# Sorting networks of a graph kernel: scalar_tensor_tensor in place of tensor_tensor, over whole 66-column slots

## The chip, the core and the metric

The kernel runs on one core of a Trainium2 chip. A core has a matrix engine (TensorE; PE in the profile, its weight loads PEld), a vector engine (VectorE, DVE), an activation engine (ScalarE, ACT), a general engine (GpSimd, POOL), which here starts the gathers, and SyncE (SP), which starts plain DMAs. Each engine works through its own list of instructions in a fixed order; semaphores order the engines among each other, and also an instruction behind an earlier one of the same engine where the data ask for it. The metric is the device time of one execution in microseconds (us).

## The reference, cut to what matters

Input are 16 batches of a graph with 1024 nodes and 64 channels, with a sparse adjacency matrix (about 16 neighbours to a node). Four layers follow each other, each ending in a residual and a layer normalisation:

- Layer 0: `x + adj @ (x @ W) + b`.
- Layer 1: neighbours are thinned out (a node with more than 10 neighbours loses one or two of them, and they lose it), and then, for every node and channel, the values of the kept neighbours and of the node are **sorted**, and three interpolated quantiles of them are added with weights. A small network of two matrix products follows.
- Layer 2: an embedding, three rounds of `relu(adj @ (h @ W + b))`, and a projection.
- Layer 3: `t = adj @ x`, of which only `t > 0.5` is used.

The sort of layer 1 is what the change touches:

```
vals = jnp.where(valid[..., None], x[:, None, :, :], big)
sv = jnp.sort(vals, axis=2)
...
for tau, wt in zip(TAUS, QWEIGHTS):
    q = gather(lo) * (1.0 - frac) + gather(hi) * frac
    agg = agg + wt * q
```

## The kernel before

**Tiles and groups.** Each batch's 1024 nodes are put into an order by their number of kept neighbours and cut into eight tiles of 128 nodes, one node to a partition. A tile with its longest lists needs 31, 21, 19, 17, 15, 15, 13 or 11 **slots** (`KS`). Tiles are handled in five groups (`GROUPS`): tile 0 alone with 31 slots, tiles 6 and 7 together with 13, tiles 2 and 3 with 19, tiles 4 and 5 with 15, tile 1 alone with 21. A slot of one tile is a row of `R` = 66 float32 columns to a partition: the 64 channels of a neighbour (`C` = 64) and two columns that hold which two neighbours the thinning takes out there. With two tiles in a group their rows for the same slot lie next to each other.

**Steps of one group.** `gathered` (L808) fetches the rows: one indirect DMA on POOL for each slot and tile (L815), 129 to a batch with some shared ones, into a buffer `g` that comes from a ring of four. `masked` (L847) reads the two extra columns (L862) and adds a huge number to rows that don't count, on ACT (L868). `quantiles` (L891) sorts the slots by a **network**: a fixed list of minimum and maximum operations over slots (`NETS`, L72), each one DVE instruction at L906, which goes back and forth between `g` and a second buffer `s`. An entry of the list holds the operation, the buffers, and for each operand a first slot, a run of neighbouring slots, a step and a count of runs. `box` (L898) makes the access pattern of it: up to three dimensions (count, rows of the run, 64 columns), so that the two extra columns are left out. `summed` (L916) weighs the needed sorted slots on ACT (L932) and adds them up on PE (L936).

**The rest of a batch.** `words_of` (L502) loads and transposes the adjacency rows and runs layer 0; on DVE it has L526 and L527. `listing` (L587) makes the lists of neighbours; on DVE it has L646, L694, L699, L701, L707 and L710, among them two with three inputs: L694 with a constant and L710 with one number to a partition. `back` (L1122) runs the small network of layer 1 and layers 2 and 3, mostly on PE, with a layer normalisation (L383) on DVE and ACT.

**What sets the order.** All steps are Python generators that yield a planned duration after each instruction or two. A planner (L1233 to L1271) holds a queue of them by planned time, pops the earliest, lets it emit its next piece and puts it back at its time plus the yielded duration times a stretch. The order of emission is the order on every engine. Batches overlap: the five groups of a batch have planned lengths (`LENGTHS`, 192.06 in sum, the period of a batch), gathers of a group are planned two groups ahead of its network, and `back` of a batch runs beside the networks of the next. The stretch of a network makes its instructions fill the group's length; the planned durations are these:

```
yield (nt * count * run * C + 151) / 960
...
cost = 0.2 + sum((len(GROUPS[g]) * x[4] * x[8] * C + 151) / 960 for x in network(n))
add(start(q), quantiles(st, g), (start(q + 1) - start(q)) / (cost + 0.1))
```

Of the kernel before, what the change touches and what calls it, by code (L numbers as in the profile page):

```python
# [17 lines left out]
ALU = mybir.AluOpType  # L18
# [129 lines left out]

def network(n):
    return [tuple(map(int, op.split(","))) for op in NETS[n].split(";")]  # L150


@with_exitstack
def kernel(
# [18 lines left out]
    nc = tc.nc  # L173
    B, N, C = x.shape
# [7 lines left out]
    R = C + 2  # L182
# [41 lines left out]
    for c in range(T):  # L224
        for s in range(2):
            half = slice(s * W, (s + 1) * W)
            nc.vector.tensor_scalar(pow2[half, c, :W], ident[half, half], 2.0 ** (7 - 2 * c - s),
                                    None, op0=ALU.mult)
# [9 lines left out]
    for t in range(T):  # L238
        n = max(KS[u] for g in GROUPS for u in g if t in g)
# [71 lines left out]
    for i in range(S):  # L311
# [4 lines left out]
        else:  # L316
            nc.vector.scalar_tensor_tensor(bias16, piece, ident[:S, i:i + 1], bias16,
                                           op0=ALU.mult, op1=ALU.add)
# [463 lines left out]
    def group(g):  # L782

        n = max(KS[t] for t in GROUPS[g])
        lo, hi = RANKS[n]
        return GROUPS[g], n, lo, hi + 1 - lo
# [104 lines left out]
    def quantiles(st, g):  # L891
        tiles, n, lo, kw = group(g)
        nt = len(tiles)
        while ("hat", g) not in st:
            yield 0.5
        bufs = st["g", g], srt.tile([P, KMAX * R], F32, tag="y", name="s", bufs=2)

        def box(buf, first, run, step, count):  # L898
            v = buf[:, first * nt * R:]
            dims = [[step * nt * R, count]] if count > 1 else []  # L900
            dims += [[R, run * nt]] if run * nt > 1 else []
            return bass.AP(tensor=v.tensor, offset=v.offset,
                           ap=[list(v.ap[0])] + dims + [[1, C]])

        for mode, a, b, d, run, sa, sb, sd, count in network(n):
            nc.vector.tensor_tensor(box(bufs[mode >> 1 & 1], d, run, sd, count),  # L906
                                    box(bufs[mode >> 3], a, run, sa, count),
                                    box(bufs[mode >> 2 & 1], b, run, sb, count),
                                    ALU.max if mode & 1 else ALU.min)
            yield (nt * count * run * C + 151) / 960  # L910
        w = tmp.tile([P, nt, kw], F32, tag="w", name="w")
        nc.vector.tensor_reduce(w, st["hat", g].rearrange("p t s k -> p t k s"), AX.X, ALU.add)  # L912
        yield 0.2
        st["sorted", g] = bufs, w
# [334 lines left out]
    for b in range(B):  # L1249
        ready = start(b * G - 2) - BEFORE  # L1250
        add(ready - LISTS - WORDS, words_of(state[b]), WORDS / WORDS_STEPS)
        add(ready - LISTS - (LEAD if b else EARLY), front(state[b]), LISTS / LISTS_STEPS)
        add(start((b + 1) * G) + AFTER, back(state[b]), BACK / BACK_STEPS)
        for g in range(G):
            q = b * G + g
            st = state[b]
            count = sum(KS[t] for t in GROUPS[g])
            many = sum(ROWS[t].count(P) for t in GROUPS[g]) + len(packs_of(g))
            add(start(q - 2), gathered(st, g), (start(q - 1) - start(q - 2)) / (many + 1))
            half = (start(q) - start(q - 1)) * (PAIRS if len(GROUPS[g]) > 1 else MASKS)  # L1260
            add(start(q) - half, masked(st, g), 0.9 * half / (1.5 + 0.4 * count + 2.1 * len(GROUPS[g])))
            n = max(KS[t] for t in GROUPS[g])
            cost = 0.2 + sum((len(GROUPS[g]) * x[4] * x[8] * C + 151) / 960 for x in network(n))
            add(start(q), quantiles(st, g), (start(q + 1) - start(q)) / (cost + 0.1))
            add(start(q + 1) + SUMS, summed(st, g))
# [50 lines left out]
```

## Time and profile before

| | |
|---|---|
| time, median of 3 runs | 3176.69 us (3176.14 to 3177.83) |
| span of the profiled execution | 4328.2 us; the page gives no other time for it |
| busy PE, DVE, ACT, POOL in it | 2647.8, 2822.0, 1914.0, 2160.8 us |
| mean granted TensorE clock | 0.764 |
| network instructions (L906) | 3648, which is 228 to a batch |
| gathers of slots (L815, `g<-table`) | 1952, mean 1048 ns, median 947 ns |

The profiled execution is 1151.5 us longer than the median of the runs. Its rows tell what an instruction takes and what holds it; how full the engines are in an ordinary run has to be worked out by setting busy times against 3176.69 us. Busy is the union of the instructions' durations, so that instructions of one engine that overlap count once. In groups of instructions, `s<-g 128x768` means that an instruction writes 768 elements in each of 128 partitions of `s` from data in `g`.

### The profile page before, as it was taken

The page shows a single profiled execution, that of the slowest core. Times are in us where ns is not written, and L with a number is a line of the kernel's source. Part 1 is how long each engine was busy: PE and PEld are TensorE (multiplying, and loading weights), DVE is VectorE, ACT ScalarE, POOL GpSimd, SP SyncE. Part 2 cuts the span into 40 slices and gives each one's busy share as a digit, 9 for nine tenths or more (in the row PEclk, how much of TensorE's full clock was granted, in tenths as well). Part 3 has the DMA queues.
Part 4 walks back from the last instruction along what each step waited for, and adds up shares of the span by engine and source line. Part 5 has one row for each costly group of instructions (what it writes and reads, how often), then busy time and mean ns, then how long its engine had stood idle before and what let it go on. Part 6 is the DMA issues. An engine that isn't in the chain of part 4 may idle for free.

```text
span 4328.2 us, 46055 instructions
## 1 busy us (share of the span) xinstructions
PE 2647.8 (61%) x13765; PEld 1635.7 (38%) x13766; DVE 2822.0 (65%) x6935; ACT 1914.0 (44%) x6153; POOL 2160.8 (50%) x2078
## 2 busy tenths in 40 slices
PE   6034285675848567584755758476575848456478
PEld 5023152443525244352533435253343525233243
DVE  6058383865849486594857668485766859476671
ACT  2034352634536264453535455363545536253641
POOL 1715626455454645546465464546545554645600
PEclk8566597787969778796877879687787969768688
DMA  3212121322222132222213222231322222111210
GB/s 107 42 50 70 34 67 37 104 54 78 73 71 84 40 101 56 78 77 74 77 39 90 64 83 76 65 84 40 100 60 79 78 80 71 39 57 24 62 43 3
DMA packets 169056, 282.54 MB, mean 65 GB/s; under 512 B 99485, under 2 KB 102112, under 8 KB 166880
## 3 DMA queue, kind: packets, MB, share of 16 engines
q1 hardware_dynamic: 67584, 142.01, 9.9%
q0 software_dynamic: 66048, 69.88, 9.1%
q10 hardware_dynamic: 35168, 67.62, 4.1%
q8 instruction: 114, 1.87, 0.2%
q14 instruction: 142, 1.16, 0.1%
HBM read 204.33 MB, written 71.44 MB: 64 GB/s over the span
## 4 chain that ended last, share of the span: by engine, by line
another core or an unknown queue 28%; DVE 25%; PE 23%; ACT 16%; issue 7%; DMA 0%; ACTq 0%; DVEq 0%
DVE g L906 7%; PE mm L1207 7%; DVE s L906 7%; ACT g L868 6%; ACT ones_at L974 3%; PE ax L464 3%; ACT ones_at L975 2%; PE tp L439 2%; PE mm L377 2%; PE pa L936 2%; PE mm L1196 2%; ACT g L932 1%; PE mm L1141 1%; DVE top L707 1%
## 5 line engine op out<-in xcount | busy, mean ns | idle before, releaser
L815 POOL DMA_INDIRECT g<-table,idx x1952 | 2045.4, 1048 | 1919.7 <-PE pa L936 666.8
L1207 PE MATMUL mm<-adjB,msg 128*128 128x512 f32 x1536 | 769.6, 621 | 109.1 <-issue 82.4
L936 PE MATMUL pa<-g,ident 128*128 128x128 f32 (+1 forms) x1600 | 376.0, 360 | 430.1 <-ACT g L932 300.5
L868 ACT ACTIVATE g<-g,bias 128x64 f32<-128x64 f32 (+9 forms) x2272 | 596.8, 341 | 47.9 <-DVE bias L864 29.2
L906 DVE TENSOR_TENSOR s<-g 128x256 f32<-128x256 f32 (+9 forms) x944 | 531.3, 588 | 64.5 <-ACT g L868 55.5
L936 PEld LDWEIGHTS pa<-g,ident 128*128 128x128 f32 x1600 | 312.3, 248 | 574.0 <-ACT g L932 347.1
L906 DVE TENSOR_TENSOR g<-s 128x256 f32<-128x256 f32 (+8 forms) x864 | 473.4, 573 | 9.0 <-DVE s L906 3.0
L932 ACT ACTIVATE g<-g,w 128x64 f32<-128x64 f32 x1552 | 397.8, 341 | 17.2 <-DVE w L912 13.6
L1207 PEld LDWEIGHTS mm<-adjB,msg 128*128 128x128 f32 x1536 | 268.7, 197 | 301.1 <-issue 270.7
L1147 DVE TENSOR_TENSOR u<-mm,mb 128x512 f32<-128x512 f32 x32 | 22.1, 691 | 463.1 <-remote 313.5
L464 PE MATMUL ax<-at,xt 128*64 128x128 f32 x1920 | 284.5, 310 | 17.4 <-issue 17.4
L377 PE MATMUL mm<-adjB,x 128*64 128x512 f32 x512 | 272.6, 666 | 36.3 <-issue 31.3
L979 PE MATMUL mm<-ones_at,pieces 128*64 128x512 bf16 x768 | 213.0, 420 | 119.0 <-ACT ones_at L975 77.1
L464 PEld LDWEIGHTS ax<-at,xt 128*64 128x64 f32 x1920 | 250.2, 158 | 81.2 <-issue 79.1
L439 PE MATMUL tp<-ident,arow 128*128 128x128 f32 x1024 | 181.7, 309 | 156.2 <-remote 66.4
L399 DVE TENSOR_REDUCE ln_v<-sq 128x8 f32<-128x512 f32 x64 | 43.6, 681 | 296.4 <-issue 156.8
L439 PEld LDWEIGHTS tp<-ident,arow 128*128 128x128 f32 x1024 | 140.9, 162 | 205.1 <-issue 131.7
L441 ACT COPY at<-tp 128x512 f32<-128x512 f32 x240 | 139.0, 580 | 177.2 <-remote 122.3
L906 DVE TENSOR_TENSOR g<-g,s 128x256 f32<-128x256 f32 (+5 forms) x432 | 199.1, 464 | 15.1 <-remote 5.0
L906 DVE TENSOR_TENSOR g<-g 128x256 f32<-128x256 f32 (+8 forms) x304 | 200.7, 660 | 11.2 <-remote 4.0
L1219 PE MATMUL mm<-ident,tT 64*128 64x64 f32 x128 | 25.7, 295 | 293.9 <-ACT tT L380 207.4
L1210 ACT ACTIVATE hlT<-mm 128x512 f32<-128x512 f32 x96 | 57.4, 598 | 296.4 <-PE mm L1207 123.7
(225 smaller groups left out, 4361.9 us busy)
## 6 DMA issues: line engine op xcount, KB each, us to landing
arow<-in_adj_dram SPq DMA_DIRECT2D x128, 512.0 KB
adjd<-at ACTq DMA_DIRECT2D x120, 512.0 KB
adjB<-adjd SPq DMA_DIRECT2D x15, 4096.0 KB
g<-table,idx POOLq DMA_INDIRECT x1952
table<-xc ACTq DMA_DIRECT2D x16, 264.0 KB
xt<-in_x_dram SPq DMA_DIRECT2D x16, 256.0 KB
out_dram<-y SPq DMA_DIRECT2D x16, 256.0 KB
stage<-table,packed POOLq DMA_INDIRECT x112
```

The costliest lines, as they stand in the source:

```text
L377: nc.tensor.matmul(pa[:C, :], src[:, m, :], adjT[:, h * TH:(h + 1) * TH, m, :], start=(m == 0), stop=(m == T - 1))
L439: nc.tensor.transpose(pt[:, i * P:(i + 1) * P], a[:, j * P:(j + 1) * P], ident)
L441: nc.scalar.copy(at[:, h * TH:(h + 1) * TH, :], pt.rearrange("p (i n) -> p i n", n=P))
L464: nc.tensor.matmul(self.bank[:C, cols], self.xt[:, m + 1, :], at[:, m, :], start=(m == 0), stop=(m == T - 1))
L815: nc.gpsimd.indirect_dma_start(out=dst, out_offset=None, in_=st["table"], in_offset=bass.IndirectOffsetOnAxis(ap=index, axis=0))
L868: nc.scalar.activation(v, v, AF.Identity, bias=bias[:m, i, k:k + 1])
L906: nc.vector.tensor_tensor(box(bufs[mode >> 1 & 1], d, run, sd, count), box(bufs[mode >> 3], a, run, sa, count), box(bufs[mode >> 2 & 1], b ...
L932: nc.scalar.activation(slots(g, bufs[0], lo + r, lo + r + 1)[:, i, 0, :C], slots(g, bufs[at[r]], lo + r, lo + r + 1)[:, i, 0, :C], AF.Iden ...
L936: nc.tensor.matmul(pa[:, :(e - k) * nt * C], ident, rows_.rearrange("p (k c) -> p k c", c=R)[:, :, :C], start=(j == 0), stop=(j == len(run ...
L974: nc.scalar.activation(ones_at, iota, AF.Abs, bias=st["minus"][:, s:s + 1])
L979: nc.tensor.matmul(bank[:C, :], pieces[:, i, s, :], ones_at[:, h * HALF:(h + 1) * HALF], start=(s == 0 and i == 0), stop=False)
L1207: nc.tensor.matmul(pg, msg[:, m, :], adjT[:, h * TH:(h + 1) * TH, m, :], start=(m == 0), stop=(m == T - 1))
```

## The change

Each minimum or maximum of a network becomes a `scalar_tensor_tensor` that multiplies the first operand by the constant 1.0 and then takes the minimum or maximum with the second. That instruction gets at most two dimensions beside the partitions here, where the old boxes had up to three. So a box of several runs is taken over all 66 columns of its rows: rows of a run are then one stretch of `run * nt * 66` elements, and the second dimension is the count. A function `widths` goes through a network from its end and gives each operation its width: 66 where it has several runs of more than one row, or where a later operation of width 66 reads what it writes; else 64. The planned duration that a network's step yields goes by the new width; `cost`, from which the stretch is worked out, still goes by 64 columns. The two extra columns of a slot hold no more than leftovers after `masked` has read them, and nothing reads them later but the networks.

```diff
+def widths(n, nt, narrow, full):
+
+    def places(buf, first, run, step, count):
+        return {(buf, first + i * step + r) for i in range(count) for r in range(run)}
+
+    read, found = set(), []
+    for mode, a, b, d, run, sa, sb, sd, count in reversed(network(n)):
+        out = places(mode >> 1 & 1, d, run, sd, count)
+        wide = bool(out & read) or (count > 1 and run * nt > 1)
+        read -= out
+        if wide:
+            read |= places(mode >> 3, a, run, sa, count) | places(mode >> 2 & 1, b, run, sb, count)
+        found.append(full if wide else narrow)
+    return found[::-1]
...
-        def box(buf, first, run, step, count):
+        def box(buf, first, run, step, count, width):
             v = buf[:, first * nt * R:]
-            dims = [[step * nt * R, count]] if count > 1 else []
-            dims += [[R, run * nt]] if run * nt > 1 else []
-            return bass.AP(tensor=v.tensor, offset=v.offset,
-                           ap=[list(v.ap[0])] + dims + [[1, C]])
-
-        for mode, a, b, d, run, sa, sb, sd, count in network(n):
-            nc.vector.tensor_tensor(box(bufs[mode >> 1 & 1], d, run, sd, count),
-                                    box(bufs[mode >> 3], a, run, sa, count),
-                                    box(bufs[mode >> 2 & 1], b, run, sb, count),
-                                    ALU.max if mode & 1 else ALU.min)
-            yield (nt * count * run * C + 151) / 960
+            if run * nt == 1:
+                dims = [[step * R, count]] if count > 1 else []
+                dims += [[1, width]]
+            elif width == R:
+                dims = [[step * nt * R, count]] if count > 1 else []
+                dims += [[1, run * nt * R]]
+            else:
+                dims = [[R, run * nt], [1, width]]
+            return bass.AP(tensor=v.tensor, offset=v.offset, ap=[list(v.ap[0])] + dims)
+
+        for (mode, a, b, d, run, sa, sb, sd, count), width in zip(network(n), widths(n, nt, C, R)):
+            nc.vector.scalar_tensor_tensor(box(bufs[mode >> 1 & 1], d, run, sd, count, width),
+                                           box(bufs[mode >> 3], a, run, sa, count, width), 1.0,
+                                           box(bufs[mode >> 2 & 1], b, run, sb, count, width),
+                                           op0=ALU.mult, op1=ALU.max if mode & 1 else ALU.min)
+            yield (nt * count * run * width + 151) / 960
```

What the networks consist of, for one batch, and how many operations get width 66:

| group of tiles | operations | elements to a partition | of width 66 | elements added |
|---|---|---|---|---|
| 0 | 46 | 22,592 | 44 | 666 |
| 6, 7 | 34 | 11,648 | 34 | 364 |
| 2, 3 | 59 | 23,040 | 58 | 716 |
| 4, 5 | 28 | 14,336 | 28 | 448 |
| 1 | 61 | 13,120 | 59 | 384 |
| a batch | 228 | 84,736 | 223 | 2,578 |

## The prediction

> **What bounds the kernel now.** I read the page first, for what is full and what ended last.
>
> ```profile
> span 4328.2 us, 46055 instructions
> ...
> PE 2647.8 (61%) x13765; PEld 1635.7 (38%) x13766; DVE 2822.0 (65%) x6935; ACT 1914.0 (44%) x6153; POOL 2160.8 (50%) x2078
> ...
> another core or an unknown queue 28%; DVE 25%; PE 23%; ACT 16%; issue 7%; DMA 0%; ACTq 0%; DVEq 0%
> ...
> L815 POOL DMA_INDIRECT g<-table,idx x1952 | 2045.4, 1048 | 1919.7 <-PE pa L936 666.8
> ```
>
> The profiled execution is 1151.5 us longer than the median of the runs, 3176.69 us, and 28% of its span (1212 us) is time on the chain that no engine or known queue accounts for. An ordinary run can't hold that, so idle time here says little about it; busy time says more. The second view, stretches of time, cuts the span before the first network instruction (267) and behind the last (4195):
>
> ```profile
> 0.00:267.00 267.00, 86.77 (x755) 73.69 (x757) 76.81 (x284) 40.88 (x119) 107.17 (x124) 0.68 0.25 66
> 267.00:4195.00 3928.00, 2459.69 (x12692) 1512.10 (x12691) 2726.86 (x6609) 1844.63 (x5983) 2053.64 (x1954) 0.77 0.24 66
> 4195.00:4329.00 134.00, 101.29 (x318) 49.96 (x318) 18.33 (x44) 28.47 (x53) 0.00 (x0) 0.81 0.10 36
> ```
>
> (Length, then busy PE, PEld, DVE, ACT, POOL.) DVE works 2726.9 us between its first and last network instruction. An ordinary run has for that stretch 3176.7 less the 134 us tail, less a head that can't be under about 130 us: the first gather starts at 96 us and the 21 whole slots of tile 0 follow each other by 1.25 us or more. That leaves some 2910 us, 94% of which DVE is busy. I take DVE as what paces an ordinary run. POOL comes close: 2160.8 busy and 0.30 us between gathers, which the view of waits calls issue:
>
> ```profile
> POOL g L815 <- PE pa L936: 666.8, 42, 80.5
> POOL g L815 <- issue: 566.6, 1858, 0.5
> ```
>
> With 96 ahead of the first gather and about 215 behind the last (4114.7 of 4328.2) that makes 2161 + 567 + 311 = 3039 us of 3177. Its other waits are for buffers that the sorted groups free (L936), so it stands behind the networks more than ahead of them.
>
> **The change part by part.**
>
> *The instruction by itself.* Groups of DVE instructions, shapes apart:
>
> ```profile
> L906 DVE TENSOR_TENSOR s<-g 128x768 f32<-128x768 f32 x144 | 136.4, 957 | 1.2
> L906 DVE TENSOR_TENSOR g<-s 128x512 f32<-128x512 f32 x160 | 106.8, 692 | 1.6
> L906 DVE TENSOR_TENSOR s<-g 128x256 f32<-128x256 f32 x256 | 102.0, 420 | 0.7
> L694 DVE SCALAR_TENSOR_TENSOR cand<-wd,wordkey 128x512 int32<-128x512 int32 x75 | 51.4, 686 | 71.0 <-ACT wd L688 40.3 <-issue 22.4 <-ACT hat L886 4.2
> L710 DVE SCALAR_TENSOR_TENSOR kw<-cand,top 128x320 f32<-128x320 f32 x128 | 72.1, 563 | 12.9 <-DVE top L707 7.1 <-remote 1.6
> ```
>
> At 512 elements a scalar_tensor_tensor with a constant (L694) takes 686 ns, a network's tensor_tensor 692. But durations overlap; what counts is from start to start, in the timeline:
>
> ```profile
> 2290.42 0.17 DVE L407 SCALAR_TENSOR_TENSOR ln_v<-ln_v,ln_r 128x8 f32<-128x8 f32 x1
> 2290.62 0.17 DVE L408 SCALAR_TENSOR_TENSOR ln_v<-ln_v,ln_r 128x8 f32<-128x8 f32 x1
> 2290.82 0.17 DVE L409 SCALAR_TENSOR_TENSOR ln_r<-ln_v,ln_r 128x8 f32<-128x8 f32 x1
> 2290.91 0.68 DVE L906 TENSOR_TENSOR s<-g 128x512 f32<-128x512 f32 x1
> 2291.51 0.68 DVE L411 TENSOR_TENSOR y<-u,ln_r 128x512 f32<-128x512 f32 x1
> ```
>
> A 512-element tensor_tensor is followed after 0.60 us (2290.91 to 2291.51). So is L694, below (3087.08 to 3087.68). So 3648 instructions change their kind at a price of nothing. The bounds: L694 against L906 says -6 ns each (-22 us); L710, which takes a number per partition and not a constant, takes 552 ns at its median, some 66 above the 486 of a 320-element tensor_tensor (+241 us in all). L694 is the nearer row, having a constant, and I take zero; but its type is int32, and the only float32 rows with a constant and two buffers (L407 to L409) have 8 elements.
>
> One rule speaks against this part. The Trainium skill, Vector Engine (DVE) Microarchitecture Reference, section 7, says that such an instruction with two non-bf16 sources in SBUF runs at half throughput. By it the 1,397,024 elements of the changed networks would cost about 1,455 us more, an estimate, and the kernel would take about 4,630 us. The trace differs: at two cycles of 1.04 ns for each of 320 elements L710 would last over 667 ns, and it takes 552; L694 would take twice its time.
>
> *The extra columns.* 223 of a batch's 228 operations get width 66, 2,578 elements to a batch, 41,248 in all. The slope from the rows: (957 - 420) / (768 - 256) = 1.05 ns. That is 43 us of DVE time, in the networks, with no cover on DVE itself. Old three-dimensional boxes pay nothing for their extra dimension (692 ns at 512, like the plain 693 of L701 of that size), so the simpler pattern gives nothing back.
>
> *Waits among DVE instructions.* In the built programs the network instructions that wait for the one directly ahead of them on DVE go from 1168 to 1251, since boxes that didn't touch now do in the columns between. The price: L408 starts 0.20 us behind L407, for which it waits; the network instruction that doesn't wait starts 0.09 behind L409. Rows of 256 elements say 0.45 against 0.335. So 0.115 us each, 83 times, 10 us. What is queued behind each is the next DVE instruction. Waits for ACT stay at 87.
>
> *The gathers.* While POOL starts a gather inside a DVE instruction with two inputs, the gather lasts until that instruction ends:
>
> ```profile
> 2048.54 1.40 DVE L906 TENSOR_TENSOR g<-g,s 128x512 f32<-128x512 f32 x2
> 2048.67 1.35 POOL L815 DMA_INDIRECT g<-table,idx  x1 [0.30 <-issue]
> ...
> 3087.08 0.69 DVE L694 SCALAR_TENSOR_TENSOR cand<-wd,wordkey 128x512 int32<-128x512 int32 x1
> 3087.42 1.17 POOL L815 DMA_INDIRECT g<-table,idx  x1 [0.30 <-issue]
> 3087.68 0.42 DVE L699 TENSOR_SCALAR bit<-wd 128x512 int32<-128x512 int32 x1
> ```
>
> An unheld gather takes 947 ns (the median). The first began 0.13 us into a 0.67 us tensor_tensor and took 0.40 more; the second began 0.34 into a 0.69 us scalar_tensor_tensor and took 0.22 more: they end 0.81 and 0.82 us behind that instruction's end. So the new kind holds gathers just as the old one. All holding adds 1952 x (1048 - 947) = 197 us to POOL, some 165 of it by networks; a wait's mean length goes with the square of the instruction's, 1.03 x 1.03, so +10 us on POOL, beside DVE's work.
>
> *The order.* POOL and SP keep theirs. On DVE, PE and ACT steps trade places by a few, since network steps are planned up to 3% longer (2.7 us to a batch, times a stretch of 1.0 to 1.9) while `cost` stays; a network's end, and with it `summed`, is planned about a microsecond later. I put this at nothing, from -10 to +15 us: it moves what DVE does next, not what it does, and the cover is that both lists keep DVE fed.
>
> The sum on DVE is 43 + 10 = 53 us. With DVE idle for 6% of its stretch, and idle time at a group's first operations able to swallow more than its share, I let 85% through: **+45 us, 3222 us**. In the profiled execution L906 holds 7.4 + 7.1% of the chain, 628 us of the 1971 that its instructions last, so its own span would grow by a third of 53, some 17 us, to 4345; its unexplained stretches can hide that.
>
> **The rivals.**
> *POOL paces.* Then DVE's 53 us fall into idle time and +10 remains: 3187, up to 3200 where both alternate. For it: 3039 of 3177. Against: 42 waits for L936.
> *Gathers run free.* The constant's form with float32 lets go of what the gather needs. Then POOL loses up to 165 us, and as far as it paces the kernel gets faster, down to DVE's floor: 130 + 2727 + 53 + 134 = 3044, likelier about 3110. It decides if gathers that start inside network instructions come to 0.95 us. Against: L694 and L710 hold them to their ends.
> *Covered.* DVE's waits swallow it all: 3170 to 3183. Against: 94%.
> *Order goes bad.* Displaced steps make another engine wait: +15 us and more on top, 3240 to 3290.
> *Half throughput*: 4,630 by the page cited; from the rows alone at most 241 + 53, 3470.
>
> **How the numbers follow.** DVE paces, 3205 to 3238: 0.66. POOL paces, 3184 to 3200: 0.14. Covered: 0.06. Gathers free: 0.05. Order bad: 0.06. A dearer instruction (half throughput or L710's extra): 0.03. The order may also turn out lucky, 0.02 out of the first. Runs of this kernel tell 0.2% (6.4 us) from no change. Faster 0.07, same 0.06, slower 0.87. The range 3182 to 3246 holds the first two cases and some of the fourth, 8 in 10.
>
> **What would show it.** Right: network rows of 264, 528 and 792 elements at about 428, 709 and 982 ns as SCALAR_TENSOR_TENSOR; DVE busy up by some 45; gathers at a mean of 1050 to 1060 ns, those inside a network instruction still held to its end. Wrong: network rows of another slope, gathers at 950, or DVE idle behind ACT or PE where it now follows itself.

## The result and the profile after

The changed kernel takes 3224.62 us (median of 4 runs, 3223.05 to 3228.91), the kernel before beside it 3176.41 us (4 runs, 3174.85 to 3177.83). The ratio is 1.0153, with a 95% interval of 1.0139 to 1.0168: 48.2 us slower.

The profiled execution of after took 3228.91 us, with a span of 3227.2. The profile of before in the prediction (span 4328.2) is like those of a chip on which the kernel before takes 4327.57 us, while on the other chips used here it takes 3176 to 3178 us; so a profile of the unchanged kernel from one of those (called *before, second profile*; time 3173.32 us) is set beside that of after here. First its page, span, busy time and the chain that ended last:

```profile
span 3171.6 us, 46055 instructions
...
PE 2499.0 (79%) x13765; PEld 1553.5 (49%) x13766; DVE 2827.0 (89%) x6935; ACT 1900.1 (60%) x6153; POOL 2273.9 (72%) x2078
...
PE 38%; DVE 30%; POOL 12%; ACT 11%; issue 6%; DMA 3%; DVEq 0%; ACTq 0%; SPq 0%; POOLq 0%
```

The same of after:

```profile
span 3227.2 us, 46055 instructions
...
PE 2530.6 (78%) x13765; PEld 1570.5 (49%) x13766; DVE 2879.2 (89%) x6935; ACT 1901.2 (59%) x6153; POOL 2259.4 (70%) x2078
...
DVE 41%; PE 30%; ACT 11%; POOL 10%; issue 5%; DMA 2%; DVEq 0%; ACTq 0%; SPq 0%; POOLq 0%
...
L831 POOL DMA_INDIRECT g<-table,idx x1952 | 2136.6, 1095 | 761.6 <-issue 565.6
```

The unexplained 28% of the chain is gone in both. DVE is busy 52.2 us longer, POOL 14.5 us shorter, and DVE's share of the chain goes from 30% to 41% (that share measures no loss: in old_plan, below, which loses 15 us, it is 51%). The groups of after's networks, shapes apart (busy in us, mean ns of one):

```profile
L927 DVE SCALAR_TENSOR_TENSOR s<-g 128x792 f32<-128x792 f32 x144 | 140.6, 977 | 1.7
L927 DVE SCALAR_TENSOR_TENSOR g<-s 128x528 f32<-128x528 f32 x160 | 110.3, 706 | 1.6
L927 DVE SCALAR_TENSOR_TENSOR s<-g 128x264 f32<-128x264 f32 x256 | 104.1, 427 | 1.2
```

427, 706 and 977 ns stand where 428, 709 and 982 were forecast. In after the new instruction takes the old one's time for its element count; only the elements are more.

What POOL waits for (us in total, times, the longest). Before, second profile:

```profile
POOL g L815 <- issue: 570.8, 1873, 0.3
POOL g L815 <- DVE nb L527: 93.8, 2, 93.5
...
POOL g L815 <- DVE g L906: 3.0, 10, 0.3
```

After:

```profile
POOL g L831 <- issue: 565.6, 1856, 0.3
POOL g L831 <- DVE nb L542: 103.7, 3, 93.7
POOL g L831 <- DVE g L927: 43.8, 9, 7.1
...
POOL g L831 <- DVE s L927: 18.0, 7, 5.8
```

The 93 us at `nb` are the head, before the first gather. Behind it, before's POOL runs without a pause: from the first gather to the end of the last it takes 2905.3 us, of which 2064 gathers of 1100.5 ns make 2271.4, gaps of 0.30 us between them 626.0, and longer waits only 7.9. After's 2959.0 us are 2257.0 + 622.0 + 80.0. So the 53.7 us on POOL are -14.4 in gathers, -4.0 in gaps and +72.1 in waits. The timeline shows one of them, at the start of a batch in after (start, length, and in brackets the idle time ahead of it):

```profile
1931.43 1.11 POOL L831 DMA_INDIRECT g<-table,idx  x1 [0.30 <-issue]
...
1939.01 1.11 POOL L831 DMA_INDIRECT g<-table,idx  x1 [6.48 <-DVE g L927]
```

The second gather stands 6.48 us until a network is done with the buffer it will fill. About six microseconds of that kind lie ahead of the first gather of each of batches 6 to 13; before has none there.

For the rest it helps to look at a steady part, from the first gather of batch 6 (of 0 to 15) to the first gather of batch 14, eight batches. Stretches of time (length, then busy PE, PEld, DVE, ACT, POOL, the granted clock, and two DMA figures), before, second profile:

```profile
1181.80:2641.50 1459.70, 1215.34 (x6859) 752.21 (x6858) 1394.70 (x3398) 949.80 (x3077) 1140.08 (x1033) 0.91 0.35 99
```

After:

```profile
1191.90:2687.00 1495.10, 1240.51 (x6881) 764.12 (x6880) 1426.37 (x3409) 951.81 (x3082) 1127.88 (x1033) 0.89 0.34 97
```

Divided by eight, with DVE's idle time in the trace split into gaps under 150 ns (between one of its instructions and the next) and longer ones, us for a batch:

| | period | DVE busy | gaps under 150 ns | longer idle |
|---|---|---|---|---|
| before, second profile | 182.5 | 174.3 | 5.4 | 2.7 |
| after | 186.9 | 178.3 | 5.6 | 3.0 |

So in the kernel before, with the gaps counted as taken, POOL is 99.7% full between its first and last gather ((2271.4 + 626.0) / 2905.3), and DVE in the steady part 98.5% ((174.3 + 5.4) / 182.5). Both are full. That DVE's work costs time is shown by dve_more3, below; that POOL paces too is read from its fullness, and no run here shows it. After adds 4.0 us of DVE work to a batch; the period grows by 4.4, and POOL waits for the buffers.

### The profile page after: what moved, and what is told of

The parts are those of the page before. It is cut to its first block, busy times and chain, and to the rows that moved or that the text cites. A ratio compares the mean times of both kernels' runs of the same rounds, so it can differ in the third digit from the quotient of the medians.

```text
span 3227.2 us, 46055 instructions
## 1 busy us (share of the span) xinstructions
PE 2530.6 (78%) x13765; PEld 1570.5 (49%) x13766; DVE 2879.2 (89%) x6935; ACT 1901.2 (59%) x6153; POOL 2259.4 (70%) x2078
## 4 chain that ended last, share of the span: by engine, by line
DVE 41%; PE 30%; ACT 11%; POOL 10%; issue 5%; DMA 2%; DVEq 0%; ACTq 0%; SPq 0%; POOLq 0%
DVE s L927 11%; DVE g L927 11%; PE mm L1228 10%; POOL g L831 9%; PE mm L393 7%; PE ax L480 4%; DVE top L723 3%; ACT ones_at L995 3%; PE pa L957 3%; DVE kw L726 3%; ACT g L884 3%; ACT ones_at L996 2%; PE mm L1217 1%; DVE cand L710 1%; DMA g<-table,idx 1%
## 5 line engine op out<-in xcount | busy, mean ns | idle before, releaser
L831 POOL DMA_INDIRECT g<-table,idx x1952 | 2136.6, 1095 | 761.6 <-issue 565.6
L927 DVE SCALAR_TENSOR_TENSOR s<-g 128x264 f32<-128x264 f32 (+9 forms) x944 | 545.6, 604 | 6.5
L927 DVE SCALAR_TENSOR_TENSOR g<-s 128x264 f32<-128x264 f32 (+10 forms) x864 | 484.4, 584 | 3.4
L393 PE MATMUL mm<-adjB,x 128*64 128x512 f32 x512 | 246.6, 610 | 5.0 <-DVE x L427 4.8
L927 DVE SCALAR_TENSOR_TENSOR g<-g 128x264 f32<-128x264 f32 (+8 forms) x304 | 205.3, 675 | 6.7
L927 DVE SCALAR_TENSOR_TENSOR g<-g,s 128x264 f32<-128x264 f32 (+6 forms) x432 | 204.7, 474 | 7.3
L1000 PEld LDWEIGHTS <-pieces 128*64 128x64 bf16 x768 | 88.8, 117 | 195.7 <-issue 136.1
L902 ACT ACTIVATE hat<-iota,npos 128x10 f32<-128x10 f16 (+2 forms) x384 | 113.9, 297 | 102.3 <-DVE npos L891 102.3
L667 PE MATMUL wd<-hi,perm 128*128 128x71 f16 x960 | 100.0, 221 | 86.6 <-DVE perm L662 86.6
L927 DVE SCALAR_TENSOR_TENSOR s<-s,g 128x264 f32<-128x264 f32 (+4 forms) x400 | 151.3, 382 | 6.2
```

Of the source, the lines that this page charges most:

```text
L393: nc.tensor.matmul(pa[:C, :], src[:, m, :], adjT[:, h * TH:(h + 1) * TH, m, :], start=(m == 0), stop=(m == T - 1))
L667: nc.tensor.matmul(pw[:, :hn], ws, hi[:, t, :], start=False, stop=False)
L831: nc.gpsimd.indirect_dma_start(out=dst, out_offset=None, in_=st["table"], in_offset=bass.IndirectOffsetOnAxis(ap=index, axis=0))
L902: nc.scalar.activation(h, iota[:, lo:lo + kw], AF.Abs, bias=npos[:, i, s:s + 1])
L927: nc.vector.scalar_tensor_tensor(box(bufs[mode >> 1 & 1], d, run, sd, count, width), box(bufs[mode >> 3], a, run, sa, count, width), 1.0, ...
L1000: nc.tensor.matmul(bank[:C, :], pieces[:, i, s, :], ones_at[:, h * HALF:(h + 1) * HALF], start=(s == 0 and i == 0), stop=False)
```

## The experiments

The theory of the prediction is that the 48 us are DVE work, most of it the extra columns. Its rivals: the kind of instruction costs them; the order costs them, which the longer planned durations bring; or POOL paces and the cost comes by way of the gathers. Later runs ask how much work the idle time of DVE swallows. A run's comparison is always with the kernel before on the same chip.

### before_again: the kernel before once more

> The kernel before, unchanged, for a profile to set beside that of the changed one (span 3227.2 us). The profile shown of before was 1151.5 us longer than its median; if that lay with that one execution, this span is near 3175 us. Theory A (DVE paces): DVE busy some 94% between first and last network instruction, 45 to 55 us less in all than the 2879.2 after. Theory B (POOL paces): gathers at a mean near 1070 ns here against 1095 after, and POOL filled between its first and last gather.

This and the next three ran on a chip where the kernel before takes 4327.57 us (median of 23 runs, 4298.57 to 4348.41). Its page there:

```profile
span 4355.3 us, 46055 instructions
...
PE 2678.1 (61%) x13765; PEld 1644.0 (38%) x13766; DVE 2823.9 (65%) x6935; ACT 1911.2 (44%) x6153; POOL 2132.3 (49%) x2078
```

The profile on which the prediction was made was thus an ordinary one of such a chip, and not a stray execution, and the expected span near 3175 us did not come. DVE is idle for 35% of the span there, so small costs on DVE can hide; its busy time says what work a change adds, the time on this chip says less.

### kind_only: the new instruction for half of the network

Boxes that already had at most two dimensions, 1808 of 3648, become `scalar_tensor_tensor`; columns and planned durations stay.

```diff
-            nc.vector.tensor_tensor(box(...), box(...), box(...), ALU.max if mode & 1 else ALU.min)
+            if count > 1 and run * nt > 1:
+                nc.vector.tensor_tensor(out, in0, in1, pick)
+            else:
+                nc.vector.scalar_tensor_tensor(out, in0, 1.0, in1, op0=ALU.mult, op1=pick)
```

> The new kind of instruction alone: scalar_tensor_tensor with the constant 1.0 wherever the old 64-column box has at most two dimensions (1808 of 3648 network instructions), tensor_tensor at the rest, all boxes and the plan as before. If the kind costs nothing: within 5 us of before. If it gets L710's extra 66 ns: +119 us. If it lets go of what gathers need: up to -80 us.

Measured: 4326.33 us, ratio 1.0003 (0.9974 to 1.0032); DVE busy 2823.7 against 2823.9. Both kinds stand side by side in its groups, shapes apart:

```profile
L911 DVE TENSOR_TENSOR s<-g 128x256 f32<-128x256 f32 x176 | 69.8, 420 | 0.6
L913 DVE SCALAR_TENSOR_TENSOR s<-g 128x256 f32<-128x256 f32 x80 | 32.2, 419 | 0.1
...
L911 DVE TENSOR_TENSOR g<-g,s 128x512 f32<-128x512 f32 x96 | 65.2, 679 | 1.2
L913 DVE SCALAR_TENSOR_TENSOR g<-g,s 128x512 f32<-128x512 f32 x32 | 21.9, 684 | 0.6
```

419 against 420 ns and 684 against 679: no price, float32 and with a constant. The Trainium skill, Vector Engine (DVE) Microarchitecture Reference, section 7, says half throughput for two non-bf16 sources in SBUF; these rows show none of it.

### width_only: columns and order, with the old instruction

After, with `tensor_tensor` put back:

```diff
-            nc.vector.scalar_tensor_tensor(box(...), box(...), 1.0, box(...),
-                                           op0=ALU.mult, op1=ALU.max if mode & 1 else ALU.min)
+            nc.vector.tensor_tensor(box(...), box(...), box(...), ALU.max if mode & 1 else ALU.min)
```

> The new boxes and the new plan, but tensor_tensor in them: 41,248 elements more, 83 more waits on the instruction directly ahead, same order as the changed kernel. If the kind costs nothing: all of the +48 us, between +44 and +52. If the kind carries part of it, as much less.

Measured: 4400.43 us, ratio 1.0162 (1.0128 to 1.0197), DVE busy 2877.7, that is 53.8 more than before_again. The slowdown of the whole change is there without the new instruction, 1.62% against 1.53%. In us it is 72.9, more than the 44 to 52 expected, on a chip where an execution takes longer.

### order_only and order_only2: the order alone

Old boxes and old instructions; only the planned duration goes by the new widths. Every instruction and every operand is that of before, in another order: in the built programs, that of after on every engine.

```diff
-        for mode, a, b, d, run, sa, sb, sd, count in network(n):
+        for (mode, a, b, d, run, sa, sb, sd, count), width in zip(network(n), widths(n, nt, C, R)):
...
-            yield (nt * count * run * C + 151) / 960
+            yield (nt * count * run * width + 151) / 960
```

> The old boxes and the old kind, but planned durations by the new widths: the order of the changed kernel with the work of the old. By the prediction nothing, -10 to +15 us. If displaced steps carry part of the result, clearly over +5 us.

Measured on the chip of 4327.57 us: 4345.58, 18.0 us more, ratio 1.0038 (1.0002 to 1.0073). That is little and near the edge of what can be told there, so the same kernel ran again as order_only2 on a chip where before takes 3178.21 us (9 runs):

> Old boxes, old kind, planned durations by the new widths, once more, for a chip that runs the kernel before at 3177 us. The changed kernel at the old plan measured +15 there and the changed kernel +48, so 33 us stand to the order's account. Theory C (the order costs by itself: 83 more waits on the instruction directly ahead, 10 us, and DVE reaching L694 and L1222 before their inputs): +10 to +33 us. Theory D (the order costs only where the wider boxes have used up DVE's slack): 0 to +8 us.

Measured: 3201.83 us, ratio 1.0077 (1.0063 to 1.0090), **+23.6 us** for nothing but an order. Its page (lines stand 16 further down than in before, so L710 is before's L694 and L1238 before's L1222):

```profile
span 3201.4 us, 46055 instructions
...
PE 2515.6 (79%) x13765; PEld 1564.9 (49%) x13766; DVE 2841.9 (89%) x6935; ACT 1901.7 (59%) x6153; POOL 2244.2 (70%) x2078
```

DVE is busy 14.9 us longer than in the second profile of before, though it does the same work. In the built programs 1251 network instructions wait for the DVE instruction directly ahead of them, as in after; in before 1168. At the prediction's 0.115 us the 83 are 10 us of the 15. They come from the order and not, as the prediction has it, from boxes that touch in the columns between: the kernels below with wide boxes and the old planned durations have 1168. The rest of its loss in the steady part is idle time of DVE, 0.9 us a batch more than in before, all of it at two places (before's rows for them stand under old_plan):

```profile
DVE cand L710 <- ACT wd L704: 19.1, 8, 2.4
DVE u L1238 <- PE mm L1235: 7.9, 8, 1.8
```

### before_again2, dve_more and pool_more: which engine has room

before_again2 is the second profile shown above, on a chip where before takes 3175.87 us (19 runs).

> The kernel before, unchanged, once more for its profile. If the chip runs it at about 3177 us, the profile can be set beside that of the changed kernel (3227.2): DVE busy 45 to 55 us less than 2879.2, its share between first and last network instruction near 94%. Theory A (DVE paces): POOL has some 3% of waits between its first and last gather. Theory B (POOL paces): POOL has none but its 0.30 us between gathers.

Measured: 3173.32 us. Of the two theories, B has the waits right: 7.9 us of longer waits in 2905.3 are 0.3%, not 3%. A has DVE right: 52.2 us less than in after.

dve_more adds 128 instructions to DVE, eight to a batch, whose results nobody reads:

```diff
-        for mode, a, b, d, run, sa, sb, sd, count in network(n):
+        for j, (mode, a, b, d, run, sa, sb, sd, count) in enumerate(network(n)):
+            if j % 27 == 13:
+                nc.vector.max(out=extra, in_=wide_ident)
```

> The kernel before with 8 more DVE instructions to a batch among the network's, 128 in all: a maximum over 256 constants, with one input, whose result nobody reads. Gathers that start inside such an instruction of L707 aren't held (946 ns). Each takes about 0.33 us from start to start, 43 us in all. Theory A (DVE paces): +30 to +45 us at 3177. Theory B (POOL paces): +0 to +10 us.

Measured: 3181.03 us, ratio 1.0017 (1.0007 to 1.0026), +5.2 us, for 32.7 us of DVE work (2859.7 against 2827.0). That is the figure that theory B gave, but the idle time explains it without B: in the steady part a batch has 2.6 us more DVE work, 1.3 us less idle time, and a period 1.1 us longer. dve_more3, below, tells the two apart.

pool_more adds 464 instructions to POOL, one behind every fourth gather:

```diff
             gather(buf[:, (k * nt + i) * R:(k * nt + i + 1) * R], st["idx"][:, t, k:k + 1])
+            if j % 4 == 3:
+                nc.gpsimd.memset(extra, 0.0)
```

> The kernel before with one small instruction more on POOL after every fourth gather, some 450 in all, each perhaps 0.1 to 0.4 us with what lies between, 45 to 180 us of POOL time and none of DVE's. Theory A (DVE paces): under +15 us. Theory B (POOL paces): the whole of what POOL's busy time and gaps grow by.

Measured: 3181.57 us, ratio 1.0017 (1.0007 to 1.0026), +5.7 us, with POOL busy 71 us longer (2345.0), 62.4 of them the memsets. The memsets went into the 0.30 us between gathers, where POOL is not busy by the profile: from first to last gather the gaps take 628.4 us against 626.0. What lengthened are the gathers (mean 1106.0 ns against 1100.5, 11.5 us). As a test of whether POOL paces this is inconclusive, since it hardly lengthened what was to be lengthened.

### old_plan and width_old_plan: the columns alone

old_plan is after with the planned durations of before; in the built programs the order on every engine is then that of before, and what remains is the columns and the kind.

```diff
-            yield (nt * count * run * width + 151) / 960
+            yield (nt * count * run * C + 151) / 960
```

> The changed kernel, with the planned durations of before (64 columns): new kind, new boxes, old order of emission. If the order carries nothing: +44 to +52 us against before. If the order of the changed kernel costs something, less by that.

Measured: 3191.18 us, ratio 1.0055 (1.0038 to 1.0072), +15.3 us. DVE is busy 39.1 us longer than in before_again2:

```profile
span 3187.4 us, 46055 instructions
...
PE 2513.2 (79%) x13765; PEld 1565.9 (49%) x13766; DVE 2866.1 (90%) x6935; ACT 1903.4 (60%) x6153; POOL 2248.8 (71%) x2078
```

width_old_plan is the same with `tensor_tensor` for all 3648.

> Wide boxes at the old plan, but with tensor_tensor. At the new kind this measured +15 us. If the kind costs nothing: +12 to +19. If the kind carries the rest: near 0.

Measured: 3191.12 us, ratio 1.0044 (1.0029 to 1.0059), +12.9 us beside before on another chip; DVE busy 2866.0 against old_plan's 2866.1. That settles the kind for all 3648 instructions: 0.1 us of DVE work. And of the columns' 39 us of DVE work a third comes through as time. Part of the rest is covered at the start: the first gather of batch 6 begins at 1179.4 us in old_plan and at 1181.8 in before. What DVE waits for in the steady part tells where another part went. Before, second profile:

```profile
DVE cand L694 <- ACT wd L688: 15.4, 8, 2.1
...
DVE u L1222 <- PE mm L1219: 4.3, 8, 0.8
```

old_plan, in which the wait of `u` for PE has gone from the steady part:

```profile
DVE cand L710 <- ACT wd L704: 11.4, 8, 1.4
...
POOL g L831 <- DVE s L927: 39.0, 10, 5.7
```

After:

```profile
DVE cand L710 <- ACT wd L704: 15.3, 8, 2.0
...
DVE u L1243 <- PE mm L1240: 8.4, 8, 1.6
...
POOL g L831 <- DVE g L927: 32.0, 5, 7.1
POOL g L831 <- DVE s L927: 16.8, 3, 5.8
```

The columns make DVE later at `cand` and `u`, whose inputs from ACT and PE are then ready sooner before it comes: idle time falls from 2.7 to 1.4 us a batch (table below), which pays for 1.3 of the columns' 3.1 us. In after's order DVE comes to both places ahead of their inputs again: 15.3 and 8.4 us in eight batches, though it has more work than old_plan.

### plan_105: another order

The kernel before, with the planned duration of a network's step 5% longer; nothing else.

```diff
-            yield (nt * count * run * C + 151) / 960
+            yield 1.05 * (nt * count * run * C + 151) / 960
```

> The kernel before with planned durations of the networks times 1.05, nothing else: again another order of emission, with 1141 waits on the instruction directly ahead in place of 1168 (1251 in the changed order). If the waits carry what an order costs: -3 to +3 us. If any longer plan makes DVE reach other steps too early: +10 us and more.

Measured: 3204.68 us, ratio 1.0088 (1.0073 to 1.0103), **+26.5 us**. Here 1141 network instructions wait for the one directly ahead, fewer than in before, and DVE's busy time grows by 5.8 us only (2832.8). So the cost of this order is not in those waits. DVE's waits in the steady part:

```profile
DVE cand L694 <- ACT wd L688: 26.7, 8, 3.4
```

11.3 us more in eight batches than before's 15.4, at the same place. A larger part of the loss lies ahead of the steady part, whose first gather begins at 1200.2 us against 1181.8. On POOL the 2905.3 us from first to last gather become 2935.0: 24.4 of the 29.8 are gathers, at a mean of 1112.3 ns, 0.9 fewer are gaps and 6.3 are waits. Two orders of the same work, order_only2's and this one, each cost about 25 us, the one with late buffers (70.0 us of POOL waits), the other with longer gathers and few waits (14.2).

The granted TensorE clock, 0.860 to 0.870 in the runs of after, is no rival for such costs: plan_105 loses its 26.5 us at 0.873 to 0.875, where before has 0.870 to 0.877 beside it, and the four runs of old_plan, at 0.866 to 0.879, lie within 4.1 us of each other.

### dve_more3: when the room is used up

dve_more with `if j % 9 == 4`, 416 extra instructions instead of 128.

> As the run with 128 DVE instructions more, which measured +5 us, but with 416 of them, 26 to a batch. In the steady batches of that run DVE was busy 0.325 us more for each, and its idle time fell by 1.35 us to a batch. Theory E (both engines are full: the gathers pace until DVE's last 1.4 us of idle time to a batch is used, then DVE paces in full): 8.45 us more to a batch less 1.4, some +7 us to a batch, +80 to +110 us in all. Theory F (DVE's work mostly hides behind the gathers): three times +5, some +15 to +30 us.

Measured: 3241.93 us against 3175.98 (7 runs), ratio 1.0212 (1.0193 to 1.0231), +65.9 us, for 114.7 us of DVE work: between the ranges of the two theories, nearer to E. The steady part:

```profile
1196.90:2702.30 1505.40, 1237.18 (x6882) 766.46 (x6881) 1457.23 (x3619) 954.93 (x3082) 1113.33 (x1032) 0.90 0.34 96
```

The first 2.6 us of work a batch (dve_more) lengthened the period by 1.1; the next 5.3 by 4.6. What can be swallowed is some 1.5 to 2 us of idle time a batch; beyond that work counts nearly whole there. Over the execution less than that comes through, since the first three batches have periods of 176 to 182 us in before, after and dve_more3 alike: extra work there is still covered.

All readings of the steady part, us for a batch, and POOL's waits from first to last gather of the whole execution:

| | time against before | period | DVE busy | gaps | longer idle | POOL waits |
|---|---|---|---|---|---|---|
| before_again2 | | 182.5 | 174.3 | 5.4 | 2.7 | 7.9 |
| dve_more | +5.2 | 183.6 | 176.9 | 5.3 | 1.4 | 39.4 |
| width_old_plan | +12.9 | 184.3 | 177.5 | 5.5 | 1.4 | 47.1 |
| old_plan | +15.3 | 184.3 | 177.4 | 5.5 | 1.4 | 51.0 |
| order_only2 | +23.6 | 185.4 | 176.1 | 5.6 | 3.6 | 70.0 |
| plan_105 | +26.5 | 184.0 | 174.3 | 5.3 | 4.4 | 14.2 |
| after | +48.2 | 186.9 | 178.3 | 5.6 | 3.0 | 80.0 |
| dve_more3 | +65.9 | 188.2 | 182.2 | 5.2 | 0.85 | 121.1 |

## Why the prediction was right, and where it was wrong

Its time, 3222 us against 3224.62, is right; two of the steps that lead to it are not, and that their errors cancel is luck: for the columns alone its reckoning gives 43 x 0.85 = 37 us, where 13 to 15 were measured.

- **"DVE paces", "POOL comes close": half right.** The 94% hold as an average, but in the steady part DVE is 98.5% full and POOL 99.7% from first to last gather. Both are full. The sum of 3039 us for POOL failed first of all at its busy time, taken from the stretched profile: 2160.8 us there, 2273.9 here, since the 1952 gathers of slots have a mean of 1097 ns and not 1048 (97 us of the 113). Where DVE's instructions lie closer, they hold more gathers: of all 2064, 801 began outside any DVE instruction in the profile of the prediction, 103 in the second. The 42 waits for L936, by which the prediction set POOL behind the networks, belong to the first profile; in the second POOL waits there four times, for 0.3 us each. That the chain's 28% of unknown time can't be part of a run of 3176 us was right.
- **The kind at nothing: right.** 0.1 us of DVE work over 3648 instructions, old_plan against width_old_plan. The bound of +241 us from L710 and the half throughput fall. The prediction read L407 to L409 as its only float32 rows with a constant; its list also had L1222, 690 ns at 512 elements, though one input of that is a result of PE.
- **43 us of DVE work for the columns: right.** 39.1 measured; the slope of the rows holds to 5 ns at 792 elements.
- **Waits among DVE instructions, 10 us: the size about right, the cause wrong.** All 83 come from the order. With the old planned durations the wide boxes have none of them.
- **Gathers held alike, +10 us on POOL: the hold right, the sum wrong.** The mean is 1095 ns in after and 1097 in before; the rival of free gathers asked for something near 950. A gather that starts inside a network instruction ends a median of 0.82 us behind it in both kernels (behind its end, not at it as the prediction first says). But the sum of gathers fell by 14 us, instead of growing by 10, and the forecast mean of 1050 to 1060 ns, reckoned from the first profile, missed.
- **"The order. I put this at nothing, from -10 to +15 us": this step failed.** Alone it costs 23.6 us, outside the bounds. Its ground, that it moves what DVE does next and not what it does, holds for the work and not for the waits: an order decides whether DVE reaches `cand` and `u` before ACT and PE are done, how many network instructions follow what they need, and in which instructions gathers start.
- **"I let 85% through": this step failed too, for the columns.** Of their 39 us 13 to 15 come through, a third. In before's order the first six batches take their share without loss, and in the steady part half of the 2.7 us of longer idle time in a batch is taken up by the later DVE. Behind the new order the columns cost more: 48.2 less 23.6, 24.6 us.

Of the 48.2 us, then, the columns alone are 13 to 15 and the order alone 24. The two together cost some 10 more than the sum, and those 10 can be put to neither. They do not arise in the steady part, where the period grows by 1.8 and 2.9 us for the one and the other and by 4.4 for both, but ahead of it: the first gather of batch 6 begins at 1179.4 us in old_plan, 1182.6 in order_only2 and 1191.9 in after, against 1181.8 in before. The first batches cover either alone and not both. The rival *order goes bad*, given 0.06, had part of the mechanism, and not the time; *POOL paces* had the fuller engine right but not the sum, since the added DVE work came back to POOL as 72 us of waits for buffers.

What stays open: the two orders were compared whole. That DVE comes to `cand` and `u` too early is read from the waits; no run moved those two steps alone. What covers extra work in the first batches was not tested. Why plan_105's gathers take longer than order_only2's (1112 against 1086 ns) was not separated either.

## What to carry to other kernels

Where steps are emitted by planned durations, a changed duration is part of the change and can cost more than the work that it stands for: here, each alone, 24 us for an order against 13 to 15 for columns, so try the new operation first with the old plan. When two engines are both full, the first microseconds of extra work are paid by the idle time at single steps and what follows counts nearly whole in the steady part; a pass-through share worked out from a mean over the execution says neither. Durations may be taken from a stretched execution, but a mean that depends on how densely another engine works, such as that of held gathers, may not.

## What the runs showed of the hardware that was not expected

One chip of the same type runs the same kernel before in 4327.57 us (23 runs) and not in 3176, with a granted clock of 0.764 against 0.872, while DVE's busy time is the same (2823.9 and 2827.0 us). Nothing here tells why.

A `memset` behind every fourth gather on POOL, 464 of 134 ns, adds 62.4 us of work and only 2.4 us to the gaps between gathers: nearly half of the 0.30 us that stand there as issue is time in which POOL can work.
